# Two conv blocks on one core: a reordered combined stage, and a residual summed by an accumulating transfer

## The chip, the cores and the metric

The kernel runs on one core of a Trainium2 chip. A core has TensorE (PE: matmuls, with PEld for its weight loads), VectorE (DVE), ScalarE (ACT), GpSimd (POOL) and SyncE (SP, which here only issues transfers). They run side by side, each takes its own instructions in a fixed order, and they wait for each other on semaphores. The metric is the device time of one execution in microseconds; lower is better.

## The reference

Two residual layers over a batch of 8 images of 384 channels and 64 x 64 points, in float32:

```
x = x + L0(gn(x))        # gn: group norm, 32 groups, no scale
x = x + L1(gn(x))

L0: q, k, v = conv1x1(x, Wq|Wk|Wv); q, k = rope_2d(q), rope_2d(k)
    q = elu(q * scale) + 1; k = elu(k) + 1            # 6 heads of 64
    out = q (k^T v) / (q . sum(k) + 1e-6)             # linear attention
    return conv1x1(out, Wfc)
L1: t = conv1x1(x, w_in)
    t = irfft2(rfft2(8x8 patches of t) * fft_filter)
    t = depthwise_conv3x3(t, w_dw); x1, x2 = split(t)
    return conv1x1(gelu(x1) * x2, w_out)
```

## The kernel before

An image is held as 8 bands (`NBAND`) of 512 points; a band of x is a tile of 128 partitions x 3 x 512 (channels in three groups of 128), 768 KB. The work alternates between two stages.

*Queries* of image b (`queries`): for each band, the query projection `pq` with its rotation and elu (`q_project`), the normaliser `pn`, its reciprocal `rn` and its spreading over channels `prb` (`q_normalise`, `q_spread`), and the output projection `pf`, which adds the residual of layer 0 into x in place (`project_out`). At its start `kv_finish` turns the three accumulated key banks `acc` into one matrix `mt` (through `kx`, `pr`, `pt`, `pv`, `kvt_bd` and `pm`).

*Combined stage* (the loop over `j` at the end of the kernel function): layer 1 of image b, band by band, beside the key half of layer 0 of image b + 1. Layer 1 of a band is
- `expand_filter`: group norm on ScalarE (`hf`), w_in (`pi`, copied to `ht`), the transform of 8x8 patches (`pd`), times the filter on VectorE (`tf`);
- `back_transform`: inverse transform (`pb`), copied by ScalarE into one of two ring buffers with a halo of one row; GpSimd copies the halo rows between the two rings (L657, L658), so a band's convolution can begin only after the next band's back transform;
- `depthwise_gate`: 9 taps for 3 channel groups, the first tap of each on ScalarE (L670), the 24 others on VectorE (`dw`, L672), then Gelu on ScalarE and two products on VectorE (`gated`, L677 and L678); there is one `gated` buffer;
- `contract`: w_out (`pw`), the residual added by VectorE into the tile of x (L689), and the store of that tile from SP's queue (L690).

The key half of a band is `project` (four token groups, each with `pk` and a transpose `px`; rotation on VectorE; elu as Relu, a table load, Exp on ScalarE and L334 on VectorE; results `kc` and `xk`) and `accumulate` (`acc`, 12 matmuls into three banks). In the first three iterations no project stands beside layer 1 (bands 0 and 1 are projected before the loop); project(j - 1) runs from j = 3, and accumulate(j - 2) from j = 4. The loop has 10 iterations: layer 1's last band needs `depthwise_gate(7)` at j = 8 and `contract(7)` at j = 9. `stream_stats` takes the group-norm sums of image b + 2 from a second load of its bands (`xs`, ScalarE, L167). `load_x(b + 1, j)` follows `contract(b, j - 2)` in iteration j (L136, SP's queue).

Tiles come from pools that hand out the buffer that was freed first: `xp` (10 buffers, tiles of x), `work` (10 buffers: `hf`, `ht`, `tf`, `xk`, `kc`, `ks`, `dw`, `xs`, `qc`, `qs`, `kx`, some weights), `psum` (8 banks, of which `acc` holds three through the combined stage), `qp` (2 buffers for the tables `tk` and `tq`). A scheduler sets the order on each engine when the program is built: it takes the instructions in the order of the code as their priority, and puts a later one first where it reckons that the earlier one would wait. On the chip the order is fixed.

`norm_chain` (small matmuls `ps_m`, `ps_mc`, `ps_v`, `ps_r` with small VectorE steps between) gives the group norm's scale; `run` steps several chains in turn.

Of the kernel before, what the change touches and what calls it, by code (L numbers as in the profile page):

```python
# [12 lines left out]
ALU = mybir.AluOpType  # L13

P = 128
# [95 lines left out]
def conv_blocks_kernel(ctx: ExitStack, tc: tile.TileContext, a: dict, out: bass.AP, nb: int):  # L111
# [35 lines left out]
    def stream_stats(b, j):  # L147

        if b >= nb:
            return  # L150
        t = w_tile([P, CT, BT], f"xs_{b}_{j}")
        nc.sync.dma_start(t, x_in[b][:, :, j * BT : (j + 1) * BT])
        if j == 0:
            first = small.tile([P, CT, 6], F32, tag="first", name=f"first_{b}")
            mv = small.tile([P, CT, 2], F32, tag="mv0", name=f"mv0_{b}")
            shift = small.tile([P, CT], F32, tag="shift", name=f"shift_{b}")
            sums = small.tile([P, CT, 2, NBAND - 1], F32, tag="sums", name=f"sums_{b}")
            for m in range(CT):
# [194 lines left out]
    def k_bias(b, params, wk):  # L353

        minus_mean = params[2]
        p_ = ps_tile(f"pbk_{b}")
        for t in range(CT):
            nc.tensor.matmul(
                p_[:, :C],
                minus_mean[:, t : t + 1].to_broadcast([P, P]),  # L360
                wk[:, t, :],
                start=(t == 0),
                stop=(t == CT - 1),
            )
        parts = small.tile([QC, C], BF16, tag="kbias", name=f"kbias_{b}")
        rest = small.tile([QC, C], F32, tag="krest", name=f"krest_{b}", bufs=1)
        nc.vector.tensor_add(rest, p_[:QC, :C], bk_bc[:QC, :])
        nc.vector.tensor_copy(parts, rest)
        second, third = slice(32, 64), slice(64, QC)
        nc.vector.tensor_sub(rest, rest, parts)  # L370
        nc.vector.tensor_copy(parts[second, :], rest[second, :])
        nc.vector.tensor_copy(parts[third, :], rest[third, :])
        nc.vector.tensor_sub(rest[third, :], rest[third, :], parts[third, :])
        nc.vector.tensor_copy(parts[third, :], rest[third, :])
        return parts
# [73 lines left out]
    def kx_accumulate(b, j, kf, xk, acc):  # L449

        for i in range(4):
            for m in range(CT):
                nc.tensor.matmul(  # L453
                    acc[m][:, : C + 1],
                    kf[:, i, m * P : (m + 1) * P],
                    xk[:, i, :],
                    start=(j == 0 and i == 0),
                    stop=(j == NBAND - 1 and i == 3),
                )

    def kv_finish(b, acc, params, vb, wv, wfc):

# [139 lines left out]
        band_stats(b, j, 1, xt[b, j])  # L602


    def expand_filter(b, j, params):
        h = normalised(b, j, params, (8, 8), "f")
        ht = w_tile([P, 4, C], f"ht_{b}_{j}")
        tf = w_tile([P, 4, C], f"tf_{b}_{j}")
        for i in range(4):
            p_ = ps_tile(f"pi_{b}_{j}_{i}")  # L610
            for t in range(CT):
                nc.tensor.matmul(  # L612
                    p_[:, :C],
                    h[:, t, i * P : (i + 1) * P],
                    w_in[:, t, :],
                    start=(t == 0),
                    stop=(t == CT - 1),
                )
            nc.scalar.copy(ht[:, i, :], p_[:, :C])  # L619

        for s in range(2):
            p_ = [ps_tile(f"pd_{b}_{j}_{2 * s + i}") for i in range(2)]
            for above in range(2):
                for i in range(2):
                    nc.tensor.matmul(  # L625
                        p_[i][halves[above], :C],
                        dft[halves[i], :],
                        ht[halves[i], 2 * s + above, :],
                        start=True,
                        stop=True,  # L630
                    )
            for i in range(2):
                nc.vector.tensor_mul(tf[:, 2 * s + i, :], p_[i][:, :C], filt)  # L633
        return tf

    def back_transform(b, j, tf):
        t = ring[j % 2]
# [40 lines left out]
        nc.vector.tensor_mul(g[64:P, 1, :], g[64:P, 1, :], af[64:P, 2, :])  # L678

    def contract(b, j):  # L680
        g = gated
        x_ = xt.pop((b, j))
        for m in range(CT):
            p_ = ps_tile(f"pw_{b}_{j}_{m}")
            for s in range(2):
                nc.tensor.matmul(  # L686
                    p_, w_out[:, s, m * P : (m + 1) * P], g[:, s, :], start=(s == 0), stop=(s == 1)
                )
            nc.vector.tensor_add(x_[:, m, :], p_, x_[:, m, :])  # L689
        nc.sync.dma_start(x_out[b][:, :, j * BT : (j + 1) * BT], x_)  # L690

    k_runs = ((0, 0, C),)

    def layer0_chain(b, prepared):

        if b >= nb:
            return
        wk = load_weight(b, "wk", k_runs)
        params = []
        for _ in norm_chain(b, 0, params):  # L700
            yield
        scale_weight(wk, params)
        yield
        prepared += params, wk, k_bias(b, params, wk)

    def run(*chains):

# [4 lines left out]
    class Keys:  # L712
# [7 lines left out]

        def project(self, j):
            if self.live and j < NBAND:
                return k_project(self.b, j, self.wk, self.bias, self.kf)
            return iter(())

        def accumulate(self, j):
            if self.live and 0 <= j < NBAND:
                if j == 0:
                    self.acc = [ps_tile(f"acc_{self.b}_{m}") for m in range(CT)]
                kx_accumulate(self.b, j, *self.kf.pop(j), self.acc)  # L730

        def prepare(self, j):

# [5 lines left out]
                self.wv, self.wfc = (load_weight(self.b, n, k_runs) for n in ("wv", "wfc"))  # L739
                self.vbias = v_bias(self.b, self.params, self.wv)  # L740

    def queries(b, keys):

        params, wq, qbias, wv, wfc, vbias = keys.params, keys.wq, keys.qbias, keys.wv, keys.wfc, keys.vbias
        q = {j: q_project(b, j, wq, qbias) for j in range(2)}
        mt = kv_finish(b, keys.acc, params, vbias, wv, wfc)
        prepared = []
        chain = layer0_chain(b + 1, prepared)
        last = NBAND - 2
        for j in range(last):  # L750
            rn = q_normalise(b, j, q[j])
            q[j + 2] = q_project(b, j + 2, wq, qbias)
            if j >= 2:
                next(chain, None)
            q_spread(b, j, q[j], rn)
            if j >= 1:
                project_out(b, j - 1, q.pop(j - 1), mt)
                next(chain, None)
            if j in (4, 5):
                load_x(b + 1, j - 4)  # L760
        rn = [q_normalise(b, j, q[j]) for j in (last, last + 1)]
        project_out(b, last - 1, q.pop(last - 1), mt)
        for i in range(2):
            q_spread(b, last + i, q[last + i], rn[i])
        run(chain)
        for j in (last, last + 1):
            project_out(b, j, q.pop(j), mt)
        return prepared
# [3 lines left out]
    prepared = []  # L772
    run(layer0_chain(0, prepared))
    keys = Keys(0, prepared)
    for j in range(NBAND + 1):
        run(keys.project(j))
        keys.accumulate(j - 1)
        keys.prepare(j)
        if j < NBAND:
            stream_stats(1, j)  # L780

    for b in range(nb):
        prepared = queries(b, keys)
        keys = Keys(b + 1, prepared)
        params = []
        run(norm_chain(b, 1, params), keys.project(0))
        run(keys.project(1))
        for j in range(NBAND + 2):
            if j < NBAND:
                tf = expand_filter(b, j, params)  # L790
            if j >= 2:
                contract(b, j - 2)
                if j < NBAND:
                    load_x(b + 1, j)
            if j < NBAND:
                back_transform(b, j, tf)
            if j >= 3:
                run(keys.project(j - 1))
            keys.accumulate(j if j < 2 else j - 2 if j > 3 else NBAND)
            keys.prepare(j)  # L800
            if 1 <= j <= NBAND:
                depthwise_gate(b, j - 1)
            if j < NBAND:
                stream_stats(b + 2, j)


# [39 lines left out]
```

## Time and profile before

| what | value |
|---|---|
| median of 3 runs | 3833.22 us (3827.56 to 3851.21) |
| the profiled execution: time, span | 3833.62 us, 3831.6 us |
| granted TensorE clock, mean | 0.979 |
| PE busy | 3623.4 us, 95% of the span |
| DVE busy | 2954.4 us, 77% |
| ACT busy | 1479.3 us, 39% |
| POOL busy | 114.3 us, 3% |
| moved by DMA | 285.27 MB, of which SP's queue 281.04 MB |
| first `pi` of a combined stage to the first `pq` of the next queries | 279.4 us (1306.3 to 1585.7) |
| those queries, up to the next first `pi` | 187.2 us (1585.7 to 1772.9) |

A profile is one execution. "Busy" counts what an engine executes; matmuls overlap, so a row's duration is longer than the distance between its start and the next, and in this document distances are taken from start to start. In a row of waits the columns are the engine and line that waited, whom it waited for, the sum in us, how often, and the longest. In a row of the timeline: start, duration, engine, line, operation, output<-inputs, shape, count, and in brackets the idle time before it with what ended it. Issues of transfers stand as SPq.

### The profile page before, as it was taken

Reading aid. Unit: us, or ns where it says so; the run is one execution under the profiler, and the core shown is the slowest. Engines: PE = TensorE matmul, PEld = TensorE weight load, DVE = VectorE, ACT = ScalarE, POOL = GpSimd, SP = SyncE. Lnnn points to the kernel's source line nnn. Section 1 sums busy time; section 2 is a strip of 40 time slices with the busy share of each in tenths; the row PEclk is TensorE's granted clock in tenths of the full one; section 3 lists DMA queues with packets and bytes.
Section 4 is the critical chain, followed back from the end, with each engine's and each line's share of the span. In section 5 each row is a group of like instructions: output and inputs, shape, how many; then the busy total and the mean of one; then the engine's idle time right before and its main releaser. Section 6 shows DMA issues by size and latency. Waiting matters only on the chain.

```text
span 3831.6 us, 39602 instructions
## 1 busy us (share of the span) xinstructions
PE 3623.4 (95%) x15386; PEld 1998.2 (52%) x15386; DVE 2954.4 (77%) x4648; ACT 1479.3 (39%) x2278; POOL 114.3 (3%) x302
## 2 busy tenths in 40 slices
PE   6999999999999999999999999999999999999986
PEld 3644565455554555445554455544555445554453
DVE  4487788867878588895887868878688786887698
ACT  2421553225631365313552145521564214442142
POOL 0000000000000000000000000000000000000010
PEclk9999999999999999999999999999999999999997
DMA  5211233111231122311232113221132211221001
GB/s 187 98 67 33 81 99 108 65 48 60 98 120 56 53 83 91 107 56 42 83 114 94 45 50 100 89 94 45 58 99 101 86 34 34 74 84 67 9 25 41
DMA packets 123969, 285.27 MB, mean 74 GB/s; under 512 B 26325, under 2 KB 36742, under 8 KB 115590
## 3 DMA queue, kind: packets, MB, share of 16 engines
q1 hardware_dynamic: 120832, 281.04, 22.0%
q8 instruction: 121, 1.98, 0.2%
q10 hardware_dynamic: 2950, 1.71, 0.2%
q14 instruction: 66, 0.54, 0.0%
HBM read 232.39 MB, written 50.33 MB: 74 GB/s over the span
## 4 chain that ended last, share of the span: by engine, by line
PE 64%; DVE 25%; ACT 7%; issue 2%; DMA 1%; POOL 0%; ACTq 0%; DVEq 0%
DVE dw L672 15%; PE pf L597 13%; PE pq L529 12%; PE pk L423 9%; PE pw L686 7%; PE acc L453 7%; PE pi L612 4%; PE pb L642 3%; ACT unread L167 2%; DVE kc L334 2%; DVE kc L445 1%; PE px L425 1%; PE pn L565 1%; DVE tf L633 1%; PE pm L511 1%
## 5 line engine op out<-in xcount | busy, mean ns | idle before, releaser
L672 DVE SCALAR_TENSOR_TENSOR dw<-ring,w_dw,dw 128x512 f32<-128x512 f32 x1536 | 1079.0, 746 | 23.8 <-ACT dw L670 16.0
L453 PE MATMUL acc<-xk,kc 128*128 128x385 f32 x1536 | 528.4, 496 | 40.9 <-DVE kc L334 40.9
L423 PE MATMUL pk<-wk,x 128*128 128x384 f32 x1536 | 550.6, 493 | 0.0
L597 PE MATMUL pf<-qc,mt 128*128 128x512 f32 x1152 | 516.1, 604 | 13.2 <-DVE qc L591 13.2
L612 PE MATMUL pi<-w_in,hf 128*128 128x384 f32 x1536 | 510.2, 488 | 1.4 <-ACT hf L327 1.4
L529 PE MATMUL pq<-x,wq 128*128 128x512 f32 x1152 | 508.6, 597 | 0.0
L686 PE MATMUL pw<-gated,w_out 128*128 128x512 f32 x768 | 380.0, 630 | 64.9 <-DVE gated L677 42.3
L453 PEld LDWEIGHTS acc<-xk,kc 128*128 128x128 f32 x1536 | 289.0, 193 | 245.1 <-issue 74.3
L612 PEld LDWEIGHTS pi<-w_in,hf 128*128 128x128 f32 x1536 | 290.1, 191 | 196.8 <-issue 3.8
L423 PEld LDWEIGHTS pk<-wk,x 128*128 128x128 f32 x1536 | 290.3, 193 | 162.0 <-issue 29.4
L332 ACT ACTIVATE qs<-qc 128x1536 f32<-128x1536 f32 x64 | 95.0, 1484 | 713.1 <-DVE qc L556 713.1
L597 PEld LDWEIGHTS pf<-qc,mt 128*128 128x128 f32 x1152 | 216.6, 192 | 274.2 <-issue 247.8
L529 PEld LDWEIGHTS pq<-x,wq 128*128 128x128 f32 x1152 | 214.8, 190 | 260.8 <-issue 253.3
L426 ACT COPY xk<-px 128x384 f32<-128x384 f32 x256 | 121.2, 474 | 564.6 <-PE px L425 562.9
L436 DVE TENSOR_TENSOR kc<-pk,tk 128x384 f32<-128x384 f32 x256 | 141.7, 554 | 219.2 <-PE pk L423 218.5
L686 PEld LDWEIGHTS pw<-gated,w_out 128*128 128x128 f32 x768 | 144.5, 198 | 261.8 <-issue 127.5
L633 DVE TENSOR_TENSOR tf<-pd,filt 128x384 f32<-128x384 f32 x256 | 132.9, 548 | 145.0 <-PE pd L625 144.4
L619 ACT COPY ht<-pi 128x384 f32<-128x384 f32 x256 | 121.1, 475 | 305.0 <-PE pi L612 304.5
L167 ACT ACTIVATE unread<-xs,shift 128x512 bf16<-128x512 f32 x294 | 212.3, 722 | 23.4 <-DMA xs<-in_x 17.2
L642 PEld LDWEIGHTS pb<-idft,tf 128*128 128x128 f32 x1536 | 186.5, 192 | 54.9 <-DVE tf L633 30.1
L649 ACT COPY ring<-pb 128x512 f32<-128x512 f32 x192 | 108.7, 587 | 266.3 <-PE pb L642 265.6
L689 DVE TENSOR_TENSOR x<-pw,x 128x512 f32<-128x512 f32 x192 | 132.0, 689 | 100.6 <-PE pw L686 100.6
(128 smaller groups left out, 3861.9 us busy)
## 6 DMA issues: line engine op xcount, KB each, us to landing
tq<-in_tq SPq DMA_DIRECT2D x64, 1024.0 KB, 4.8
x<-in_x SPq DMA_DIRECT2D x64, 768.0 KB, 4.8
tk<-in_tk SPq DMA_DIRECT2D x64, 768.0 KB, 4.3
out_dram<-x SPq DMA_DIRECT2D x64, 768.0 KB, 3.5
xs<-in_x SPq DMA_DIRECT2D x56, 768.0 KB, 6.0
wk<-in_wk SPq DMA_DIRECT2D x8, 576.0 KB, 5.1
wv<-in_wv SPq DMA_DIRECT2D x8, 576.0 KB, 3.9
wfc<-in_wfc SPq DMA_DIRECT2D x8, 576.0 KB, 3.8
```

What stands on the lines that cost most here:

```text
L167: nc.scalar.activation(unread, t[:, m, :], func, bias=shift[:, m : m + 1], accum_out=sums[:, m, k, j - 1 : j])
L423: nc.tensor.matmul(pk[:, :C], tokens(t), wks[:, t, :], start=False, stop=(t == CT - 1))
L436: nc.vector.tensor_mul(chans(kc[:, i, :], 0, half), chans(pk[:, :C], 0, half), table(0, 0, QC))
L453: nc.tensor.matmul(acc[m][:, : C + 1], kf[:, i, m * P : (m + 1) * P], xk[:, i, :], start=(j == 0 and i == 0), stop=(j == NBAND - 1 and i = ...
L529: nc.tensor.matmul(p_, wqs[:, t, m * P : (m + 1) * P], xt[b, j][:, t, :], start=(t == 0), stop=(t == CT - 1),)
L597: nc.tensor.matmul(p_, mt[:, t, m * P : (m + 1) * P], q[:, t, :], start=(t == 0), stop=(t == CT - 1))
L612: nc.tensor.matmul(p_[:, :C], h[:, t, i * P : (i + 1) * P], w_in[:, t, :], start=(t == 0), stop=(t == CT - 1),)
L633: nc.vector.tensor_mul(tf[:, 2 * s + i, :], p_[i][:, :C], filt)
L642: nc.tensor.matmul(patches[:, k // 2, k % 2], tf[:, k, m * P : (m + 1) * P], idft.rearrange("p (u n) -> p u n", u=2), start=True, stop=True,)
L672: nc.vector.scalar_tensor_tensor(acc[:, m], src, wd, acc[:, m], ALU.mult, ALU.add)
L686: nc.tensor.matmul(p_, w_out[:, s, m * P : (m + 1) * P], g[:, s, :], start=(s == 0), stop=(s == 1))
L689: nc.vector.tensor_add(x_[:, m, :], p_, x_[:, m, :])
```

## The change

Six edits, all in the order of work and in the residual of layer 1:

- `contract`: ScalarE copies the product from PSUM into a new tile `y` of the work pool; a transfer from GpSimd's queue adds the tile of x to `y` in SBUF (`accum_op`), and a second one, from the same queue, stores `y`. VectorE's addition and SP's store go.
- `kx_accumulate` and `expand_filter` become chains with a point to pause at after each token group, and after `pi`.
- In each iteration of the combined stage, the key work (`fill`) is stepped between `pi`, `pd` and `back_transform`, and `contract(j - 2)` comes after it; before, `contract` stood ahead of `back_transform`, and the key work after it.
- The loop has 9 iterations; `depthwise_gate` of band 7 is called in the next queries after `kv_finish`, and `contract` of band 7 after the first `project_out` there (after the last image, at the end).
- The accumulation of band 7's keys moves into the queries, between the projections of bands 0 and 1.
- The group norm chain ahead of the combined stage is stepped between the token groups of two key projections, not of one.

```
     def contract(b, j):
-        g = gated
         x_ = xt.pop((b, j))
+        y = w_tile([P, CT, BT], f"y_{b}_{j}")
         for m in range(CT):
             p_ = ps_tile(f"pw_{b}_{j}_{m}")
             for s in range(2):
                 nc.tensor.matmul(
-                    p_, w_out[:, s, m * P : (m + 1) * P], g[:, s, :], start=(s == 0), stop=(s == 1)
-                )
-            nc.vector.tensor_add(x_[:, m, :], p_, x_[:, m, :])
-        nc.sync.dma_start(x_out[b][:, :, j * BT : (j + 1) * BT], x_)
+                    p_, w_out[:, s, m * P : (m + 1) * P], gated[:, s, :], start=(s == 0), stop=(s == 1)
+                )
+            nc.scalar.copy(y[:, m, :], p_)
+        nc.gpsimd.dma_start(y, x_, accum_op=ALU.add)
+        nc.gpsimd.dma_start(x_out[b][:, :, j * BT : (j + 1) * BT], y)
...
+    def chain_of(*chains):
+        for c in chains:
+            yield from c
...
-    def queries(b, keys):
+    def queries(b, keys, gate, output):
         params, wq, qbias, wv, wfc, vbias = keys.params, keys.wq, keys.qbias, keys.wv, keys.wfc, keys.vbias
-        q = {j: q_project(b, j, wq, qbias) for j in range(2)}
+        q = {0: q_project(b, 0, wq, qbias)}
+        run(keys.accumulate(NBAND - 1))
+        q[1] = q_project(b, 1, wq, qbias)
         mt = kv_finish(b, keys.acc, params, vbias, wv, wfc)
+        gate()
...
                 project_out(b, j - 1, q.pop(j - 1), mt)
                 next(chain, None)
+            if j == 1:
+                output()
...
-        prepared = queries(b, keys)
+        prepared = queries(b, keys, gate, output)
         keys = Keys(b + 1, prepared)
         params = []
-        run(norm_chain(b, 1, params), keys.project(0))
-        run(keys.project(1))
-        for j in range(NBAND + 2):
+        chain, first, second = norm_chain(b, 1, params), keys.project(0), keys.project(1)
+        for _ in range(4):
+            next(chain)
+            next(first, None)
+        for _ in range(2):
+            next(second, None)
+        run(chain)
+        run(second)
+        for j in range(NBAND + 1):
+            fill = chain_of(keys.project(j - 1 if j > 2 else NBAND), keys.accumulate(j if j < 2 else j - 2 if j > 3 else NBAND))
             if j < NBAND:
-                tf = expand_filter(b, j, params)
+                tf = []
+                layer1 = expand_filter(b, j, params, tf)
+                next(layer1)
+                next(fill, None)
+                run(layer1)
+                next(fill, None)
+                next(fill, None)
+                back_transform(b, j, tf[0])
+            run(fill)
             if j >= 2:
                 contract(b, j - 2)
                 if j < NBAND:
                     load_x(b + 1, j)
-            if j < NBAND:
-                back_transform(b, j, tf)
-            if j >= 3:
-                run(keys.project(j - 1))
-            keys.accumulate(j if j < 2 else j - 2 if j > 3 else NBAND)
             keys.prepare(j)
-            if 1 <= j <= NBAND:
+            if 1 <= j < NBAND:
                 depthwise_gate(b, j - 1)
             if j < NBAND:
                 stream_stats(b + 2, j)
+
+        def gate(b=b):
+            depthwise_gate(b, NBAND - 1)
+
+        def output(b=b):
+            contract(b, NBAND - 1)
+
+    gate()
+    output()
```

More of the change, by code (lines that the diff above doesn't have):

```diff
@@ L459, in kx_accumulate @@
                 )
+            yield
     def kv_finish(b, acc, params, vb, wv, wfc):
@@ L602, in project_out, with expand_filter @@
         band_stats(b, j, 1, xt[b, j])
-    def expand_filter(b, j, params):
+    def expand_filter(b, j, params, done):
         h = normalised(b, j, params, (8, 8), "f")
@@ L619, in expand_filter @@
             nc.scalar.copy(ht[:, i, :], p_[:, :C])
+        yield
         for s in range(2):
@@ L633, in expand_filter @@
                 nc.vector.tensor_mul(tf[:, 2 * s + i, :], p_[i][:, :C], filt)
-        return tf
+        done.append(tf)
     def back_transform(b, j, tf):
@@ L722, in project @@
             if self.live and j < NBAND:
-                return k_project(self.b, j, self.wk, self.bias, self.kf)
-            return iter(())
+                yield from k_project(self.b, j, self.wk, self.bias, self.kf)
         def accumulate(self, j):
@@ L729, in accumulate @@
                     self.acc = [ps_tile(f"acc_{self.b}_{m}") for m in range(CT)]
-                kx_accumulate(self.b, j, *self.kf.pop(j), self.acc)
+                yield from kx_accumulate(self.b, j, *self.kf.pop(j), self.acc)
         def prepare(self, j):
@@ L774, in conv_blocks_kernel, with nothing @@
     keys = Keys(0, prepared)
-    for j in range(NBAND + 1):
+    for j in range(NBAND):
         run(keys.project(j))
-        keys.accumulate(j - 1)
+        run(keys.accumulate(j - 1))
         keys.prepare(j)
-        if j < NBAND:
-            stream_stats(1, j)
+        stream_stats(1, j)
+    keys.prepare(NBAND)
+    def nothing():
+        pass
+    gate = output = nothing
     for b in range(nb):
-        prepared = queries(b, keys)
+        prepared = queries(b, keys, gate, output)
         keys = Keys(b + 1, prepared)
         params = []
-        run(norm_chain(b, 1, params), keys.project(0))
-        run(keys.project(1))
-        for j in range(NBAND + 2):
-            if j < NBAND:
-                tf = expand_filter(b, j, params)
+        chain, first, second = norm_chain(b, 1, params), keys.project(0), keys.project(1)
[8 more added lines that the diff above has]
+            fill = chain_of(keys.project(j - 1 if j > 2 else NBAND), keys.accumulate(j if j < 2 else j - 2 if j > 3 else NBAND))
+            if j < NBAND:
+                tf = []
[7 more added lines that the diff above has]
+            run(fill)
             if j >= 2:
@@ L794, in conv_blocks_kernel @@
                     load_x(b + 1, j)
-            if j < NBAND:
-                back_transform(b, j, tf)
-            if j >= 3:
-                run(keys.project(j - 1))
-            keys.accumulate(j if j < 2 else j - 2 if j > 3 else NBAND)
             keys.prepare(j)
-            if 1 <= j <= NBAND:
+            if 1 <= j < NBAND:
                 depthwise_gate(b, j - 1)
```

## The prediction

> **What bounds the kernel now.** I read the page first, then who TensorE waits for, then one band of the combined stage instruction by instruction.
>
> ```profile
> PE 3623.4 (95%) x15386; PEld 1998.2 (52%) x15386; DVE 2954.4 (77%) x4648; ACT 1479.3 (39%) x2278; POOL 114.3 (3%) x302
> ...
> L689 DVE TENSOR_TENSOR x<-pw,x 128x512 f32<-128x512 f32 x192 | 132.0, 689 | 100.6 <-PE pw L686 100.6
> ...
> x<-in_x SPq DMA_DIRECT2D x64, 768.0 KB, 4.8
> ...
> out_dram<-x SPq DMA_DIRECT2D x64, 768.0 KB, 3.5
> ```
>
> TensorE is busy 95% of the span, so only what leaves it idle, or slows its clock, moves the time. The waits of TensorE between 844 and 1307 us (one image: combined stage, then queries) are:
>
> ```profile
> PE acc L453 <- DVE kc L334: 5.6, 2, 3.2
> PE ps_r L280 <- DVE rsg L309: 3.1, 1, 3.1
> PE pw L686 <- DVE gated L678: 2.1, 2, 1.0
> PE pf L597 <- DVE qc L591: 1.6, 1, 1.6
> PE pd L625 <- ACT ht L619: 1.4, 1, 1.4
> ```
>
> About 16 us of some 465 per image. A steady band (1017.7 to 1053.7) is nearly dense:
>
> ```profile
> 1034.47 7.93 PE L453 MATMUL acc<-xk,kc 128*128 128x385 f32 x24
> 1042.24 7.90 PE L612 MATMUL pi<-w_in,hf 128*128 128x384 f32 x24
> 1050.07 1.52 PE L625 MATMUL pd<-ht,dft 64*64 64x384 f32 x16
> ...
> 1053.70 4.56 PE L686 MATMUL pw<-gated,w_out 128*128 128x512 f32 x10 [1.05 <-DVE gated L678]
> ```
>
> From start to start: acc 7.77, pi 7.83, pd 1.45, pw 5.15, pb 2.68, four key groups (pk with px) at 2.43 = 9.72; together 34.6 of the 36.0 us that the band takes. Gaps cost a second time: after the 3.2 us wait that ends at 1109.04 the granted clock is half.
>
> ```profile
> 1109.00:1115.00 6.00, 5.96 (x13) 0.72 0.01 3
> 1110.50:1113.50 3.00, 3.00 (x6) 0.50 0.00 0
> ```
>
> The column ahead of the last two is the clock: 6.0 x (1 - 0.72) = 1.7 us lost. The waits over 3 us are followed by such a window in most images.
>
> **The rotation of x, before.** The x pool holds ten tiles: when contract(j-2) runs, the eight bands of this image less those already stored, and the next image's, fill all of them. So x of the next image's band j can only be loaded into the tile that contract(j-2) gives up, and is read by project(j) one iteration later. The DMA-issuing queue shows it:
>
> ```profile
> 1023.00 0.38 SPq L690 DMA_DIRECT2D out_dram<-x  x1
> 1026.54 0.37 SPq L136 DMA_DIRECT2D x<-in_x  x1
> ```
>
> The store is issued 0.7 us after pw ends, landed 3.2 us after its issue, the load then started, and with 4.8 us it was there near 1031. TensorE asks for it at 1060.9 (the next band's pk): 30 us to spare.
>
> **The change, part by part.** In the changed program's own order a steady band on TensorE is: one acc, pi, pk0 (one more acc within), pd, pk1, pk2, pb, pk3, ten acc, pw. pw now ends the band and pi begins the next.
>
> 1. *Waits removed.* pw runs a band after its gate; acc of bands 6 and 7 lie behind other work (pw 5.15, pbv 2.1 and pq 7.74 now separate pk3 of band 7 from its acc); ps_r has three key groups ahead of it. Off: the combined stage's 10.1 (5.6+2.1+0.8+1.4+0.2), ps_r's 3.1, and 1.7 of clock after two of them in five images of seven, 2.4. Gain 15.6 us per image.
>
> 2. *The residual.* 192 VectorE adds go (132 us), 192 ScalarE copies of a 128x512 bank come (ring copies: 587 ns, 113 us). Neither is on TensorE's path by itself: VectorE is busy 29.0 of 36 us in the band, ScalarE 20.7. But the tap that VectorE's chain starts with is now queued on ScalarE behind y's first copy, and VectorE no longer fills the Relu-table-Exp time (1.48+1.28+1.48) with taps. Its loop, from pk3: kc/ks and add 3.0, ScalarE 4.3, L334 1.7, wait for the tap 1.0, sixteen taps at 0.67, two more and a wait for Gelu 4.4, taps, kc/ks and the psum bank that they free 3.1; then TensorE's pk1, pk2, pb, pk3 9.8: about 37, less overlaps 36.3. So VectorE's freed time buys nothing here; if the next item vanished this would be the bound.
>
> 3. *The transfer that frees x.* x now comes free when the accumulating transfer has landed, and that can start only after pw and y's third copy, at the band's end. Chain: pw's end to the end of y's last copy 1.6 (behind the three taps and an hf of ScalarE's queue), the transfer A, SP's issue 0.4, load 4.8: 6.8 + A. TensorE has until then one acc 0.65, pi 7.83, another acc 0.65: 9.2 in bands 5 to 7, 8.5 in band 4, 7.9 in the first and last of the six. Six x tiles per image (j = 2 to 7), for seven images, pay the difference, and nothing is queued on TensorE that could pass the waiting pk.
>    A isn't in the trace. From below: the 3.5 us of a plain store of the same bytes. From above: it reads x and y, two passes of the slowest row of this size, xs at 6.0: 12. By size, loads of 576 KB take 3.9 and of 1024 KB 4.8, 0.9 per 448 KB, so 1536 KB read take about 5.8; with 0.7 for GpSimd's start (a POOL copy of 128x198 takes 0.41 to 0.86) I take A = 6.5. Chain 13.3. Stalls: 5.4 + 4.8 + 2.2 (pbq's 1.9 lies there) + 4.1 + 4.1 + 5.4 = 26, and 1.7 of clock after each, 10: loss 36 us per image. With A = 3.5: 12; with A = 12: 69.
>
>    The Trainium skill, DMA: Bandwidth & Descriptors, section on the anatomy of a GpSimd-issued DMA, fits a plain one with 2.0 us plus bytes at 436 GB/s: an estimate of 3.8 us for 768 KB, by which the loss would be near 14 us per image. It has no term for the second operand; no row here shows one.
>
> 4. *GpSimd's and SP's queues.* 64 accumulates and 64 stores move to GpSimd. The store waits there for its accumulate, and behind it stand the next band's halo copies (L659, L660), which feed VectorE's taps. They are due only after the next pb, some 18 us after the accumulate's start: cover holds up to A near 18, so nothing. SP loses 64 stores; behind its waiting x load stand tk and xs, used a band later: nothing.
>
>    The Trainium skill, SBUF — State Buffer, speaks against GpSimd's queue: its descriptors can't be written while VectorE runs in a two-port fast mode. But VectorE's 128x1536 add takes 1752 ns, 0.88 elements per ns, and no row of VectorE runs at a multiple of that. By the row nothing; if the rule bit, one such add, 1.75 us, on each of 42 transfers, 74 us.
>
> 5. *Start of the stage.* Band 2 has no key work left to lie in front of pb: acc 1.9, pi 7.8, pd 1.45 after pb of band 1, 11.2 us, while VectorE does 18 taps (12.1), a gate, five serial taps (3.9) and tf (2.1): pb is late by 4.4.
>
> 6. *Band 7's gate in the queries.* 24 taps, 17 us, are put on VectorE after kvt_bd. rn of band 0 now stands behind 19 of them, prb waits 4.5; the psum banks for pq 3 come 1.6 late and rn of band 1 another 3.0: 9.1 per image. After that pw's 5.15 on TensorE lets VectorE catch up.
>
> 7. *The end.* The last image has no key work and no x load; its bands trade the adds for ScalarE's copies in a loop of the same length. After the last pw there come a copy 0.6, A, and a store 3.5, where there were an add 0.7 and a store: +6.5, with GpSimd's issue 9.
>
> Sum: per image -15.6 + 36 + 4.4 + 9.1 = +33.9; seven times 237; with the end +246. On the profiled execution (span 3831.6, time 3833.6, within 0.4 us of the median of 3833.2): 4080 us.
>
> **Rivals.**
> - *The cover holds* (faster). If A is under 2.4 + 1.1 = 3.5 or the load lands early (in one band of before, transfers of x landed in 3.5 to 4.9), no pk waits; and if rn's wait is passed over as well, only item 1 is left: 3833 - 7 x 15.6 + 9 = 3733. It decides at A near 3.5 with a load under 4.5. For it: the SBUF to SBUF transfer meets no HBM. Against: it reads twice what the 3.5 us store reads. 0.08.
> - *VectorE's loop, not x.* A small, items 5 and 6 as they are (13.5), and 36.3 instead of 34.6 in five bands (8): 3833 + 7 x (13.5 - 15.6 + 8) + 9 = 3883, with the clock after these gaps up to 3930. 0.14.
> - *A slow accumulate.* A = 12: 3833 + 7 x (69 + 13.5 - 15.6) + 15 = 4316; more if the engines add slowly, and above 18 the halo copies join. 0.20.
> - Main case, A from 4.5 to 9, which by the same sum is 3980 to 4205: 0.58.
>
> The range that holds 8 in 10: 3880 to 4350. Faster by over 1% (about what a measurement of this kernel can tell from none): 0.08, within 1%: 0.06, slower by over 1%: 0.86.
>
> **What would show it.** Right: TensorE's waits show pk <- DMA x<-in_x some 42 times, 2 to 6 us each; a band of 40 us or more; the granted clock's mean under 0.979; accumulates landing 5 to 8 us after issue; gated and kc gone from the waits; prb <- rn about 4 us once per image. Wrong: no wait of pk on x, accumulates landing under 4 us, or a combined stage no longer than the 279.4 us that it takes now from its first pi (1306.3) to the next pq (1585.7).

## The result and the profile after

The changed kernel takes 4030.7 us (median of 4 runs, 4023.7 to 4037.2), the kernel before beside it 3837.6 (4 runs): a ratio of 1.050, with an interval of 1.046 to 1.054. The profiled execution has a span of 4021.9 us, 190.3 more than before, and a mean granted clock of 0.960 against 0.979. The prediction was 4080, slower. Of the four runs of the first experiment below, the profiled one took 6072.8 us at a granted clock of 0.574: the ratio given there is of the other three (3798.4 to 3802.6 us), and TensorE's waits in that profile say nothing of theirs.

From the page of the changed kernel: the engines' busy time, the group of key projections, and the transfers of x and y.

```profile
PE 3662.1 (91%) x15386; PEld 2018.6 (50%) x15386; DVE 2836.6 (71%) x4456; ACT 1576.7 (39%) x2470; POOL 255.7 (6%) x430
...
L423 PE MATMUL pk<-wk,x 128*128 128x384 f32 x1536 | 588.0, 522 | 113.7 <-DMA x<-in_x 113.7
...
x<-in_x SPq DMA_DIRECT2D x64, 768.0 KB, 5.4
...
y<-x POOLq DMA_DIRECT2D x64, 768.0 KB, 5.8
out_dram<-y POOLq DMA_DIRECT2D x64, 768.0 KB, 7.0
```

VectorE lost 118 us of work, and TensorE, which does the same 15386 matmuls, is busy 39 us longer and idle 152 us longer: 190.3 in sum. The largest new item is the wait of `pk` for x, 113.7 us, which was not there before. Who TensorE waits for in one image (1846 to 2340, combined stage and queries):

```profile
PE pk L423 <- DMA x<-in_x: 15.6, 5, 4.3
PE prb L583 <- DVE rn L575: 5.2, 2, 3.3
PE acc L453 <- DVE kc L334: 5.2, 1, 5.2
PE pbv L398 <- DMA wv<-in_wv: 4.7, 1, 4.7
PE pf L598 <- DVE qc L592: 1.6, 1, 1.6
PE pb L644 <- DVE tf L635: 1.6, 1, 1.6
```

Of the waits shown for an image before, `pf` on `qc` is unchanged; `acc` on `kc` is there again, but as one wait early in the stage (1946.96) in place of two near its end (1080.8 and 1109.0 before); `gated`, `ps_r` and `pd` on `ht` are gone; four others came. One band, from the end of `pw` to the key projection of the next band, in the timeline of TensorE, GpSimd's and SyncE's queues:

```profile
2096.47 5.31 PE L688 MATMUL pw<-gated,w_out 128*128 128x512 f32 x12
...
2102.70 0.89 POOL L692 DMA_DIRECT2D y<-x  x1 [13.90 <-ACT y L691]
...
2108.49 0.37 SPq L136 DMA_DIRECT2D x<-in_x  x1
...
2108.77 0.78 POOL L693 DMA_DIRECT2D out_dram<-y  x1 [5.18 <-DMA y<-x]
...
2113.81 4.21 PE L423 MATMUL pk<-wk,x 128*128 128x384 f32 x6 [4.10 <-DMA x<-in_x]
```

`pw` hands over to the next matmul at 2101.6; 1.1 us later y's copies are done and the accumulating transfer is issued; 5.8 us later it has landed and SyncE starts the load of x; 5.3 us later `pk` runs. The chain is 12.2 us long, and TensorE had 8.1 us of other work (`acc`, 2101.78 to 2109.71): it stands for 4.1. What follows at once is half clock (columns as before, the clock third from the end):

```profile
2113.80:2117.40 3.60, 3.59 (x6) 2.08 (x7) 0.00 (x0) 0.00 (x0) 0.00 (x0) 0.50 0.25 104
```

By stages: from first `pi` to first `pq` the seven combined stages with key work take 291.5 us on average (280.3 before); the seven query stretches behind them, up to the next first `pi`, 198.4 (183.2). But work was moved from the one to the other, `acc` of band 7 (7.8 us) and `pw` of band 7 (5.15). Put back, the combined stage lost 24.2 us an image and the queries 2.2. The last stage takes 220.6 us against 207.2, and the stretch ahead of the first `pi` 372.0 against 380.1: 7 x 26.4 + 13.4 - 8.1 is the 190.

### The profile page after: what moved, and what is told of

It reads as the page before. It is cut to its first block, busy times and chain, and to the rows that moved or that the text cites. A ratio compares the mean times of both kernels' runs of the same rounds, so it can differ in the third digit from the quotient of the medians.

```text
span 4021.9 us, 39869 instructions
## 1 busy us (share of the span) xinstructions
PE 3662.1 (91%) x15386; PEld 2018.6 (50%) x15386; DVE 2836.6 (71%) x4456; ACT 1576.7 (39%) x2470; POOL 255.7 (6%) x430
## 4 chain that ended last, share of the span: by engine, by line
PE 66%; DVE 11%; DMA 11%; issue 9%; ACT 3%; POOL 0%; SPq 0%; ACTq 0%; POOLq 0%; DVEq 0%
PE pf L598 13%; PE pk L423 13%; PE pq L530 10%; PE acc L453 8%; DVE dw L674 7%; PE pi L613 6%; DMA x<-in_x 5%; DMA y<-x 5%; PE pb L644 3%; PE pw L688 3%; PE px L425 2%; PE pd L627 2%; DMA wv<-in_wv 1%; PE pk L421 1%; PE pn L566 1%
## 5 line engine op out<-in xcount | busy, mean ns | idle before, releaser
L674 DVE SCALAR_TENSOR_TENSOR dw<-ring,w_dw,dw 128x512 f32<-128x512 f32 x1536 | 1065.2, 747 | 91.7 <-ACT dw L672 83.7
L423 PE MATMUL pk<-wk,x 128*128 128x384 f32 x1536 | 588.0, 522 | 113.7 <-DMA x<-in_x 113.7
L453 PE MATMUL acc<-xk,kc 128*128 128x385 f32 x1536 | 527.9, 492 | 36.4 <-DVE kc L334 36.4
L613 PE MATMUL pi<-w_in,hf 128*128 128x384 f32 x1536 | 528.4, 502 | 15.6 <-ACT hf L327 15.6
L530 PE MATMUL pq<-x,wq 128*128 128x512 f32 x1152 | 519.2, 605 | 2.8 <-DVE qs L542 2.4
L423 PEld LDWEIGHTS pk<-wk,x 128*128 128x128 f32 x1536 | 303.6, 204 | 300.7 <-DMA x<-in_x 134.8
L613 PEld LDWEIGHTS pi<-w_in,hf 128*128 128x128 f32 x1536 | 300.5, 197 | 237.6 <-ACT hf L327 37.1
L688 PE MATMUL pw<-gated,w_out 128*128 128x512 f32 x768 | 348.3, 599 | 35.1 <-DVE gated L679 24.8
L334 DVE SCALAR_TENSOR_TENSOR kc<-kc,ks 128x1536 f32<-128x1536 f32 x64 | 112.4, 1756 | 199.8 <-ACT ks L333 199.8
L644 PE MATMUL pb<-idft,tf 128*128 128x128 f32 x1536 | 194.0, 281 | 18.0 <-DVE tf L635 17.1
```

The lines of the kernel that those rows point to most:

```text
L423: nc.tensor.matmul(pk[:, :C], tokens(t), wks[:, t, :], start=False, stop=(t == CT - 1))
L453: nc.tensor.matmul(acc[m][:, : C + 1], kf[:, i, m * P : (m + 1) * P], xk[:, i, :], start=(j == 0 and i == 0), stop=(j == NBAND - 1 and i = ...
L530: nc.tensor.matmul(p_, wqs[:, t, m * P : (m + 1) * P], xt[b, j][:, t, :], start=(t == 0), stop=(t == CT - 1),)
L613: nc.tensor.matmul(p_[:, :C], h[:, t, i * P : (i + 1) * P], w_in[:, t, :], start=(t == 0), stop=(t == CT - 1),)
L644: nc.tensor.matmul(patches[:, k // 2, k % 2], tf[:, k, m * P : (m + 1) * P], idft.rearrange("p (u n) -> p u n", u=2), start=True, stop=True,)
L674: nc.vector.scalar_tensor_tensor(acc[:, m], src, wd, acc[:, m], ALU.mult, ALU.add)
```

## The experiments

The first four part the change into its order and its contraction, and the contraction into its pieces.

**The new order alone**, with VectorE's addition and SyncE's store:

```
-        y = w_tile([P, CT, BT], f"y_{b}_{j}")
...
-            nc.scalar.copy(y[:, m, :], p_)
-        nc.gpsimd.dma_start(y, x_, accum_op=ALU.add)
-        nc.gpsimd.dma_start(x_out[b][:, :, j * BT : (j + 1) * BT], y)
+            nc.vector.tensor_add(x_[:, m, :], p_, x_[:, m, :])
+        nc.sync.dma_start(x_out[b][:, :, j * BT : (j + 1) * BT], x_)
```

> The new order, but contract as before: VectorE adds the product into x's tile and SP stores it. Theory (the accumulating transfer lies in the rotation of x): x comes free after an add and a 3.2 to 3.5 us store instead of a copy and 5.8 us, so from the end of pw to x loaded it is about 0.9 + 3.3 + 0.4 + 5.0 = 9.6 us against some 9.2 of TensorE's work; the waits of pk for x fall from 113.7 us to under 30, and the time to 3840 to 3900 us. Rival (the new order itself is what costs: VectorE's loop through tf, the gate among the queries): VectorE gets 132 us of adds back on top, and the time stays at 3980 or more.

Measured: 3800.8 us, ratio to before 0.990 (0.988 to 0.992). The order by itself is a gain of about 39 us. That is under the theory's range (3840 to 3900), and far from the rival's.

**The contraction alone**: the old order, with the changed `contract`.

> The old order, but contract as in the changed kernel: ScalarE's copy, accumulating transfer and store from GpSimd's queue. Theory: contract stands early in the iteration there, x had 30 us to spare, and 2 to 3 us more of transfer don't use that up; no wait of pk for x, 3810 to 3860 us. Rival (accumulating transfers or GpSimd's queue cost wherever they stand, by the shared port, the DMA engines or the halo copies behind them): 3900 us or more.

Measured: 3946.9 us, ratio 1.0275 (1.025 to 1.030). It missed the theory's range and lies in the rival's: the contraction costs 107 us in the old order too, where no `pk` waits for x. So it has a second way to cost time, which four runs below look for.

**The residual left out**: the changed kernel without the accumulating transfer; y is stored as it is.

```
-        nc.gpsimd.dma_start(y, x_, accum_op=ALU.add)
```

> The changed kernel without layer 1's residual: y is stored as it is, with no accumulating transfer, so that x's tile comes free two bands earlier. Theory: no wait of pk for x (113.7 us before, and some 7 us per image of half clock behind them); the waits of prb, pbv and acc stay; 3860 to 3920 us. Rival (order): 3980 or more.

Measured: 3825.0 us, ratio 0.996 (0.995 to 0.998); no wait of `pk` for x. The time is 35 us below the theory's range: without the stall the changed order loses nothing against the kernel before.

**An eleventh tile for x**, the transfer kept. The room for it comes from one buffer less for `kbias` and for the statistics of layer 0, and from writing the streamed statistics' unread output over xs:

```
-    xp = ctx.enter_context(tc.tile_pool(name="xp", bufs=10))
+    xp = ctx.enter_context(tc.tile_pool(name="xp", bufs=11))
...
-            for k, func in enumerate((AF.Identity, AF.Square)):
-                nc.scalar.activation(
-                    unread, t[:, m, :], func, bias=shift[:, m : m + 1], accum_out=sums[:, m, k, j - 1 : j]
-                )
+            nc.scalar.activation(
+                t[:, m, :], t[:, m, :], AF.Identity, bias=shift[:, m : m + 1], accum_out=sums[:, m, 0, j - 1 : j]
+            )
+            nc.scalar.activation(t[:, m, :], t[:, m, :], AF.Square, accum_out=sums[:, m, 1, j - 1 : j])
```

> The changed kernel with eleven tiles of x instead of ten (room for it from small tiles that lose their second buffer, and ScalarE's two sums that write in place). The accumulating transfer stays, but x of the next image is loaded into the tile that the contract before it gave up, a band earlier. Theory: waits of pk for x under 10 us in all, 3860 to 3930 us. Rival (the transfer costs by itself, not through x's rotation): 4000 or more.

Measured: 3828.3 us, ratio 0.997 (0.996 to 0.998), again below the theory's range. TensorE's waits over the whole run, the ones of some size:

```profile
PE prb L582 <- DVE rn L574: 40.1, 14, 3.3
PE acc L452 <- DVE kc L333: 36.4, 7, 5.2
...
PE pbv L397 <- DMA wv<-in_wv: 14.4, 7, 2.1
```

The 113.7 us of `pk` are gone, with the same 5.8 us for each accumulating transfer. The mean clock is back at 0.983 and TensorE's busy time at 3578.5. One tile more gives back 202 of the 230 us that part the changed kernel from the new order alone, and leaving the transfer out altogether only 3 more. So it is not the transfer as such that costs here; it is that x's tile waits for it, with no tile to spare. What the tile is worth without the transfer is shown by the last run below.

**The transfer in three pieces**, each behind its own copy of y: the same bytes, freed earlier.

```
             nc.scalar.copy(y[:, m, :], p_)
-        nc.gpsimd.dma_start(y, x_, accum_op=ALU.add)
+            nc.gpsimd.dma_start(y[:, m, :], x_[:, m, :], accum_op=ALU.add)
```

> The changed kernel with the accumulating transfer cut in three, one piece of 256 KB behind each of ScalarE's three copies; the rest as it is. Theory (x's tile is freed A after the last copy, and the stall of 16.2 us an image is what that is too late): the last piece is issued where the whole was and lands in about 3-4 us instead of 5.8, so every load of x starts 2-3 us earlier; pk<-x falls from 113.7 us to 20-55, and the time, with less of the half clock behind the stalls, from 4031 to 3890-3960 us. Rival (GpSimd's issue of three transfers, 0.9 us each, or the queue's fixed cost eats the gain): pk<-x 90-130 us, 4010-4060 us.

Measured: 3946.4 us, ratio 1.0275 (1.026 to 1.029), 84 us less than the changed kernel. Two waits of TensorE and the row of issues:

```profile
PE pk L423 <- DMA x<-in_x: 50.8, 29, 3.8
PE pbv L398 <- DMA wv<-in_wv: 49.6, 7, 8.5
...
y<-x POOLq DMA_DIRECT2D x192, 256.0 KB, 3.6
```

The last piece lands 2.2 us sooner than the whole, and the wait falls by 63 us, 1.5 on each of 42 loads, although the other new wait, `pbv`, grew by 20. Length of the chain sets the stall: the theory held.

**wk's reload from GpSimd's queue**, for the wait of `pbv` on wv, which the prediction doesn't have. In the changed kernel SyncE's queue and TensorE show at the end of the stage:

```profile
2126.29 0.37 SPq L346 DMA_DIRECT2D wk<-in_wk  x1
2127.34 0.34 SPq L525 DMA_DIRECT2D tq<-in_tq  x1
2127.73 0.43 SPq L346 DMA_DIRECT2D wv<-in_wv  x1
...
2136.43 3.58 PE L398 MATMUL pbv<-wv,nb 128*1 128x384 f32 x6 [4.69 <-DMA wv<-in_wv]
```

wv is issued 1.4 us behind wk, which waits for band 7's last transposes (`px`). In the kernel before, wv and wfc stood ahead of wk.

```
-            nc.sync.dma_start(t[:, :, at : at + n], w_in_dram[name][:, :, c0 : c0 + n])
+            queue = nc.gpsimd if name == "wk" else nc.sync
+            queue.dma_start(t[:, :, at : at + n], w_in_dram[name][:, :, c0 : c0 + n])
```

> The changed kernel with wk's reload issued from GpSimd's queue instead of SyncE's; the rest as it is. Theory (the wait pbv<-wv, 29.1 us, is wv standing in SyncE's queue behind wk's reload, which waits for band 7's last transposes): pbv<-wv goes to 0 and the time falls by 15-35 us, to 3995-4015 us. Rival (GpSimd's queue is worse: halo copies, the copies into ks_bd and the transfer of y stand behind wk's wait there): waits pbv gone, but prb, pb or pw longer by as much, 4020-4060 us.

Measured: 4024.7 us, ratio 1.048 (1.046 to 1.050), not told apart from the changed kernel; `pbv` still waits 25.1 us. SyncE's queue in the same place of this kernel:

```profile
2130.91 0.34 SPq L526 DMA_DIRECT2D tq<-in_tq  x1
2131.35 0.38 SPq L347 DMA_DIRECT2D wv<-in_wv  x1
```

With wk out of the way wv stands behind tq, which waits for the buffer that it shares with the key tables, until band 7's last `ks`. Neither theory nor rival: in this run wv stands behind another load that waits. Its place is not the whole of it, for wv's own load is also slower beside the others:

```profile
wv<-in_wv SPq DMA_DIRECT2D x8, 576.0 KB, 8.3
```

in the changed kernel, against 3.9 in the kernel before; with eleven x tiles, where wk is issued 9 us ahead of tq and wv, it takes 6.1 and `pbv` waits 2.0. No run takes tq out of wv's way, so how the wait divides between the place and the slower load isn't shown.

**Why the contraction costs 107 us in the old order.** Its trace shows ScalarE waiting for the streamed tile xs, which the kernel before hardly does (17.2):

```profile
ACT unread L167 <- DMA xs<-in_x: 74.0, 12, 7.3
```

and `acc` waiting for `kc` up to 9 us behind it (73.8 in sum against 40.9). Three runs tried to take the cause away, each over a different guess.

An eleventh x tile, with the edit above:

> The kernel before's order with the changed contraction (it ran at 3946.9 us), and an eleventh tile for x (made room for as in the run with eleven x in the new order). Theory: the 108 us that the contraction costs in the old order come through SyncE's queue: the load of x into the tile just freed waits for the accumulating transfer, the load of xs stands behind it, ScalarE's statistics of xs stand ahead of xk's copy and Relu and Exp, and so kc comes late (acc<-kc 73.8 us against 40.9). With an eleventh tile the load of x waits for the band before, xs comes in time: ScalarE's wait for xs falls from 74 us to below 25, acc<-kc to 35-45, and the time to 3820-3860 us. Rival: ScalarE's own three copies of 0.58 us a band and the work tile that y holds through a store of 7.5 us make the loss: nothing changes, 3920-3950 us.

Measured: 3941.7 us, 1.027 (1.025 to 1.029); ScalarE waits 77.5 us for xs. No effect.

The load of x called behind the load of xs:

```
                 contract(b, j - 2)
-                if j < NBAND:
-                    load_x(b + 1, j)
...
                 stream_stats(b + 2, j)
+            if 2 <= j < NBAND:
+                load_x(b + 1, j)
```

> The kernel before's order with the changed contraction (3946.9 us), ten x tiles, but within each band the load of x is issued behind the load of xs instead of ahead of it. Theory (xs held up by x's wait in SyncE's queue): xs no longer waits for the accumulating transfer, unless for its own work tile; ScalarE's wait for xs falls from 74 us to 10-40, the time to 3830-3880 us. Rival (x itself is too late, or y's work tile makes xs late): 3920-3960 us, with ScalarE's wait for xs as it was or a wait pk<-x of TensorE.

Measured: 3945.2 us, 1.027 (1.025 to 1.029); ScalarE waits 73.6 us. But in the trace SyncE still issues x ahead of xs in these bands (2053.65 and 2054.12): the schedule put them back, so this run tells nothing.

An eleventh work tile in place of the eleventh x:

```
-    work = ctx.enter_context(tc.tile_pool(name="work", bufs=10))
+    work = ctx.enter_context(tc.tile_pool(name="work", bufs=11))
```

> The kernel before's order with the changed contraction (3946.9 us), ten x tiles, and an eleventh work tile in the room that served for the eleventh x before. Theory: y is a ninth tile a band in a ring of ten; the tile that xs takes is one that y has held through the accumulating transfer and the store of 7.5 us (once an image SyncE's xs waits 7 us for that store), xs comes late, ScalarE's queue stands behind it and kc with it. With eleven tiles SyncE's wait for out_dram<-y ahead of xs goes to 0, ScalarE's 74 us for xs below 30, acc<-kc to about 41, and the time to 3830-3880 us. Rival: the load comes from ScalarE's three extra copies a band and the order in which pw's copies hold up ring's and xk's; then nothing changes, 3920-3960 us.

Measured: 3953.8 us, 1.029 (1.025 to 1.033). SyncE no longer waits for y's store ahead of xs, yet ScalarE waits 74.3 us for xs. A ring too short for y is not the cause. What is left shows in the timeline of this last kernel, the one with eleven work tiles: GpSimd's queue, SyncE's, ScalarE, TensorE.

```profile
2056.60 0.89 POOL L690 DMA_DIRECT2D y<-x  x1 [9.77 <-ACT y L689]
...
2062.69 0.37 SPq L136 DMA_DIRECT2D x<-in_x  x1
2063.22 0.37 SPq L152 DMA_DIRECT2D xs<-in_x  x1
...
2072.41 0.72 ACT L166 ACTIVATE xs<-xs,shift 128x512 f32<-128x512 f32 x1 [6.25 <-DMA xs<-in_x]
...
2083.09 1.62 PE L452 MATMUL acc<-xk,kc 128*128 128x385 f32 x2 [7.25 <-DVE kc L333]
```

x's load is issued when the accumulating transfer has landed, xs right behind it; ScalarE stands 6.25 us for xs with `xk`'s copy and the exponentials queued behind, and `acc` 7.25. In most other bands xs is ahead of x. With eleven x tiles the schedule moves each load of x forward, and xs of these bands is again behind a waiting one. So x was taken out of SyncE's queue, in the kernel with eleven work tiles:

```
         t = xp.tile([P, CT, BT], F32, tag="x", name=f"x_{b}_{j}")
-        nc.sync.dma_start(t, x_in[b][:, :, j * BT : (j + 1) * BT])
+        queue = nc.gpsimd if b else nc.sync
+        queue.dma_start(t, x_in[b][:, :, j * BT : (j + 1) * BT])
```

> The old order with the changed contraction and eleven work tiles (3953.8 us, ScalarE waiting 74.3 us in 12 waits for xs), with the loads of x issued from GpSimd's queue, behind y's store, instead of SyncE's. In the two runs before this one the load of xs of bands 6 and 7 still stood in SyncE's queue behind a load of x that waits for the accumulating transfer, so they left the theory untested. Theory (that place in the queue is what the contraction costs in the old order): xs is issued when its own tile is free, ScalarE's wait for xs falls from 74 us to below 30, acc<-kc from 69.8 to 36-50 us, TensorE's idle time by 8-12 us an image for six images and the half clock with it: 3850-3895 us. Rival (ScalarE's three extra copies a band are the cost, xs only what its queue shows as the wait): ScalarE's wait for xs may go, acc<-kc stays above 60 us and the time within 3930-3960 us.

Measured: 3856.4 us, 1.005 (1.003 to 1.006), 97 us less than the run with eleven work tiles. ScalarE's wait for xs is gone from its list, and of TensorE's:

```profile
PE acc L453 <- DVE kc L334: 36.8, 14, 3.5
```

The theory held. In the old order the accumulating transfer costs through SyncE's queue: a load that waits for it holds up a load that doesn't. What is left for ScalarE's extra copies and all the rest together is half a per cent.

**Band 7's gate back in the combined stage**, in the new order with VectorE's addition, to see whether the hand-over is what the order gains by:

```
-        for j in range(NBAND + 1):
+        for j in range(NBAND + 2):
...
-            if 1 <= j < NBAND:
+            if 1 <= j <= NBAND:
                 depthwise_gate(b, j - 1)
```

> The new order with VectorE's addition and SyncE's store (3800.8 us), but band 7's gate and contraction back in the combined stage, as its last two iterations, instead of in the next query stage. Theory (the hand-over of the gate is what the new order gains by): band 7's pw waits for its gate at the stage's end with little beside it, 5-12 us an image, less the 5 us an image of prb<-rn that leave the query stage: 3805-3860 us. Rival (the gain is the interleaving of layer 1's expansion with the keys, and the hand-over costs as much as it saves): 3785-3803 us, and the last stage some 5 us shorter.

Measured: 3790.0 us, ratio 0.987 (0.984 to 0.989) where the hand-over gave 0.990 (0.988 to 0.992): the intervals overlap. No gain is to be seen from the hand-over. The queries take 183.6 us an image here and 198.6 in the next run, which has it: it puts 15 us there. In this run's waits of TensorE, `prb` is no longer there, and x is:

```profile
PE pk L423 <- DMA x<-in_x: 42.7, 36, 3.4
```

**The new order, VectorE's addition and eleven x tiles**: the two edits shown.

> The new order with VectorE's addition and SyncE's store (3800.8 us), and an eleventh x tile. Theory (without the accumulating transfer a band of x is freed by a store of 3.5 us, in time for its load): no wait pk<-x in either, the time within 0.4% of 3800, 3785-3815 us. Rival (that store still frees x a little late): pk<-x of some 20-60 us was there with ten tiles and goes, 3740-3785 us. Against the changed kernel with eleven x (3828.3 us) both leave 15-90 us that ScalarE's copies and GpSimd's queue cost besides.

Measured: 3746.6 us, ratio 0.976 (0.974 to 0.978): faster than both kernels, and the rival was right. Also without the accumulating transfer the new order frees x a little late; with the tile to spare TensorE's first waits are

```profile
PE prb L582 <- DVE rn L574: 36.9, 14, 3.3
PE pb L643 <- DVE tf L634: 33.4, 18, 5.2
```

and neither `pk` on x, `acc` on `kc` nor `pbv` on wv is among them. The same order and tiles with the changed contraction took 3828.3: the 82 us between the two are what the contraction costs apart from x's tile. The eleventh tile is worth 54 us to VectorE's addition as well; so of the 230 us that the contraction costs in the new order, 148 go through x's tile and 82 don't. By the waits, 36.4 of it are `acc`, 14.4 `pbv`, some 14 `pi` on `hf` (on ScalarE, nearly all in the last stage) and 11 `pw` on `gated`, while `pb` waits 15 less; which part is due to ScalarE's copies and which to the schedule that they bring wasn't tried alone.

| us | VectorE's addition, SyncE's store | accumulating transfer, GpSimd's store |
|---|---|---|
| old order | 3837.6 | 3946.9 |
| new order | 3800.8 | 4030.7 |
| new order, eleven x | 3746.6 | 3828.3 |

## Why the prediction was right, and where it was not

The direction and the mechanism were right: `pk` waits for x, whose tile the accumulating transfer frees late, and the half clock behind each stall adds to it. The forecast of 4080 is 49 us too long, some 7 an image. Step by step:

- **Item 3, the chain.** Put at 13.3 us, measured 12.2: y's copies 1.1 (1.6 forecast), the transfer with its issue 5.8 (6.5), SyncE and the load 5.3 (5.2). The stalls in the image shown were 4.3, 0, 1.2, 2.9, 3.2 and 4.1, where 5.4, 4.8, 2.2, 4.1, 4.1 and 5.4 were forecast: 0.9 to 1.3 too much in five bands, which is about the chain's 1.1, and nothing in band 4, because another wait (`acc` on `kc`, 5.2) stood there. Over the run the stalls are 16.2 us an image where 26 were forecast. Item 3 as a whole, 36 us an image, measured 28.9 (the 202 us of the eleventh tile over seven, of which 2.1 are `pbv`, which that tile shortens too). This was the mis-sized term: A, 6.5 taken and 5.8 measured, y's copies, and band 4.
- **The two rules of the skill there.** By the fit in the Trainium skill, DMA: Bandwidth & Descriptors (anatomy of a GpSimd-issued DMA), a plain transfer of 768 KB takes an estimated 3.8 us. A plain store from GpSimd landed in 4.0 in the run without the residual, near the page's figure; the accumulating transfer took 5.8. The Trainium skill, SBUF — State Buffer (who interferes with whom), says that a transfer issued from GpSimd stalls when VectorE holds the port that its descriptors need. No run shows it: the run with 64 accumulating transfers and eleven x tiles and the run with none of them differ by 3 us. But no row of VectorE ran faster than 1.1 elements per ns there either, so the rule was not put to the test.
- **The clock.** "1.7 us after each" and 10 an image was about right: TensorE's busy time fell by 83.6 us, 11.9 an image, when the stalls of x were taken away.
- **Item 1, waits removed.** Partly wrong. `gated` and `ps_r` went as forecast, and so did the two waits of `acc` that were counted, but another wait of 5.2 us came in each of seven images: 36.4 us, where there had been 40.9. The schedule puts the first two `acc` of a band ahead of the next `pi` in one band of each image, directly behind `pw`, and there `kc` isn't ready. With VectorE's addition in the same order and eleven x tiles this wait is not there. VectorE, ScalarE and TensorE of that band show

```profile
1937.37 1.76 DVE L445 TENSOR_TENSOR kc<-kc,ks 128x1536 f32<-128x1536 f32 x1
...
1942.73 1.48 ACT L333 ACTIVATE ks<-ks 128x1536 f32<-128x1536 f32 x1
...
1945.07 1.75 DVE L334 SCALAR_TENSOR_TENSOR kc<-kc,ks 128x1536 f32<-128x1536 f32 x1
1946.96 1.62 PE L453 MATMUL acc<-xk,kc 128*128 128x385 f32 x2 [5.20 <-DVE kc L334]
```

- **Item 4, the queues.** "Nothing" was wrong in SyncE's queue. Behind a waiting load stand wv and wfc, not only tk and xs: `pbv` waits 4.2 us an image, and in the old order xs, put down at nothing for being "used a band later", is worth 97 us. The step that failed is the count of what stands behind the waiting load and how soon each is needed; for `pbv` the slower load of wv comes to it, as said. For GpSimd's halo copies "nothing" held: VectorE waits 1.7 us for them in both kernels.
- **Items 5 and 6.** `pb` is late by 1.6, not 4.4; `prb` and the banks of `pq` wait 5.6 an image, not 9.1. Both sizes were too large, the places right; the terms named in item 5, 18.1 us and a gate against 11.2, don't give 4.4 either.
- **How the errors met.** In the combined stage -10.1 - 2.4 + 36 + 4.4 = 27.9 was forecast and 24.2 measured: x about 7 and `pb` 2.8 too large, `acc` 5.2 and `pbv` 4.2 missing. In the queries 9.1 - 3.1 = 6.0 against 2.2. These have opposite signs, so the total came closer than its terms, which is luck; some 3 us an image of what the combined stage gained back are not accounted for by them. Over the run, 7 x 3.7 and 7 x 3.8 too much, 4.4 too little at the end and the 8.1 at the start, for which the sum has no term, make the 56 us between 246 and 190.
- **Item 2 and the rival of VectorE's loop.** Freed time on VectorE buys nothing: no run shows a gain from it, in the old order either. But 36.3 us a band is not a bound (its terms add up to 38.0, not to "about 37"): with the stall away, `pw` follows `pw` after 35.4 us in two bands of an image (1924.65 to 1960.04 is one, in the run with eleven x). Without the stall the time was 3828 where this rival said 3883 to 3930.
- **The rival "the cover holds"**, 3733, has its case in the runs without the stall: 3825 and 3828. Its price was off by 92 us in the first of them, where the waits of `acc`, `prb` and `pbv` come to 88.6. The upper end of the main case, 4205, comes out at 4188 by its own terms.
- **Item 7, the end.** 9 us forecast, 13.4 measured in the last stage. There `pi` waits 2.5 us for `hf` in each of five bands, ScalarE's work, which the step counted as a loop of the same length.
- **What was named as signs**: 35 waits of `pk` of 0.9 to 5.2 us (42 of 2 to 6 forecast), bands of 37.8 to 42.3 us (40 or more; 2074.47 to 2113.81, 39.3, is one), the clock down, transfers at 5.8 (5 to 8), `gated` out of the combined stages (the last one keeps 35.1), `kc` not, `prb` with 5.2 us in two waits an image (one of about 4).

## What to carry to other kernels

Where a ring of tiles has none to spare, whatever frees a tile is on the path of the next load into it, and a step that moves off a busy engine may lengthen that path: write the chain from the last reader to the first user, engine by engine and queue by queue, and compare it with the work in between. One tile more was worth 202 us here and cutting the transfer in three 84, while the engine time saved, 132 us of VectorE, showed no gain in any run. And for each load that has to wait, list what stands behind it in its queue: that cost 97 us in a place where x itself was in time.

## What the runs showed of the hardware

- An accumulating transfer in SBUF takes 5.8 us for 768 KB and 3.6 for 256 KB, so three pieces one behind the other free their source earlier than one.
- Two transfers of 768 KB started together slow each other: y's store from GpSimd took 7.0 us and x's load 5.4 in the changed kernel, where they start together (2108.49 and 2108.77), and 4.0 and 4.8 in the run without the residual, where for 61 of the 64 stores no load starts within 1.8 us. In the last run in the old order, with x's load 0.8 us behind the store in the same queue, the store took 4.0 and the load 7.8.
- The half clock came after short waits too. In the changed kernel 40 of the 46 gaps of TensorE over 3 us have a window of half clock within 6 us of their end, and 20 of the 39 between 1.5 and 3 us; of moments taken at random, 17 in 100 would have one.
